# A two-layer outlook-attention kernel on one core: layer 0's fold by SBUF to SBUF transfers instead of shift matmuls, and layer 1's contractions two steps later

## The chip, the cores and the metric

The kernel runs on one core of a Trainium2 chip. The metric is the device time of one execution in microseconds (us). Three runs of the kernel before gave 3605.92, 3610.51 and 3612.76 us; their median, 3610.51 us, is the time before.

## The reference, cut to what matters

Input x is (8, 56, 56, 384) in float32. Two layers follow one another, each with a residual: `x = x + layer(groupnorm(x))`, with 32 groups and statistics per image.

```python
# layer 0: 12 heads of 32, kernel 3x3, attention of 9 outputs over 9 inputs at each pixel
v_unf = patches of v = x @ Wv.T, padded by 1        # (b, n, 9, heads, 32)
a = (x @ Wa.T).reshape(b, n, heads, 9, 9)
attn = softmax(a * 32 ** -0.5)                      # over the 9 inputs q
out = einsum('bnhpq,bnqhd->bnphd', attn, v_unf)
canvas[:, i:i+h, j:j+w] += out[:, :, :, p]          # for the 9 outputs p = (i, j): a fold
return canvas[1:-1, 1:-1] @ Wo.T

# layer 1: 6 heads of 64, one output per pixel, so no fold
a = softmax((x @ W_attn + b_attn).reshape(B, H*W, 6, 9))
y = einsum('bpKhd,bphK->bphd', patches of x @ W_v + b_v, a)
return y @ W_proj + b_proj
```

In layer 0 a pixel's nine outputs land on its 3x3 neighbourhood, and each of them reads a 3x3 neighbourhood: weights of one pixel on another reach over 5x5. The kernel first adds up these weights (over columns, then over rows: "presum" and "fold") and applies them once to v.

## The kernel before, in words

**Layout.** Two images make a pair (`NPAIR` 4); a column of a pair is `R` = 112 rows (2 x 56). Layer 0 walks 4 x 56 = 224 columns, one a step. Eight patches of seven columns (`PX` 7) make an image's width; a patch is contracted when all the columns that reach into it are ready.

**A step of layer 0** (the loop at L677) does this, for different columns:

- `attend(c)`: three projections by `wa_t` into one of three PSUM banks (matmuls of 288 columns), each followed on DVE by a maximum (L486) and a subtraction (L487), with one piece of other work ("between") after each; then the exponential on ACT (L491), a projection by `wv_t` into a bank, its copy `v` on ACT (L498) and `v`'s write to a table in HBM (`vtab`, ACT's DMA queue), the denominator on DVE (L503 to L509) and the multiplication on POOL (L510).
- `presum(c)` for the column two steps back: on POOL, the weights of columns c-1, c and c+1 that land on the same column offset are added into `pre` (5 offsets x 12 heads, for the 9 row pairs pi, qi).
- `fold(c)` for the column three steps back, as the second of the three "between" pieces: the row part. Two matmuls with a 0/1 matrix `shift` move qi = 0 and qi = 2 up and down by one row and add them over pi - qi in PSUM (`pw`, L549); ACT copies the outer two of the five row offsets (L555) and DVE adds qi = 1 to the inner three (L556) into `wt`. `wt` is wider than a patch and zero around the middle, so that a shifted window of it is the row for a patch; L561 writes one such window per patch that the column reaches (336 windows in all) to a table in HBM, `ztab`, as five runs of 336 bytes a row, on ACT's DMA queue.
- `jobs.run`: up to two jobs from a list with due steps.

For each patch `fetch_v` reads the v rows (`vp`, two transfers) and `fetch` the weight rows (`z`, two transfers of 2352 KB, then the residual `xres`), all on SP's DMA queue. `fetch` adds ten jobs, due four steps later: four contractions (96 matmuls `pc` each, with two copies `yT` by ACT) and six output projections (`po`, DVE adds the residual, SP stores to `x1s`). So five steps of seven have two jobs and two have none.

**Layer 1** (the loop at L932) walks 32 groups of seven columns. `attend` projects one tile a step (logits and v, L777) and writes v to a table; at m = 0 `regroup` sends the logits of the group before through HBM; at m = 2 `weigh` makes the softmax (DVE, ACT, at last POOL at L824); at m = 3 `move` shifts by matmuls (`pw`), copies and writes `ztab1`, and `fetch` reads `vp` and `z` and adds the contractions, due four steps later. `load` (L718) brings a group's input at m = 4, `normed` normalises it at m = 6. Inputs `x1t` stay until the group is written out: four buffers, three of `io` and the one that was layer 0's `xres`. The weight tiles `z` are four halves of layer 0's two `z` buffers (`NZ` 4).

**What sets the order.** TensorE's instructions stay in the order of the program (`tc.keep_in_program_order`). Every other instruction is ordered, engine by engine, by a planner that estimates when each can start; DMAs too, on the queue of the engine that issues them (SP or ACT). DMAs take eight completion semaphores in turn, and a DMA waits for the one that had its semaphore before it, so the ninth waits for the first.

Of the kernel before, what the change touches and what calls it, by code (L numbers as in the profile page):

```python
# [15 lines left out]
def two_outlook_layers(  # L16
# [67 lines left out]
    WT = 2 * SX0 - E0  # L84
# [295 lines left out]
    def layer0(late, pools):  # L380
# [6 lines left out]
        stats, st1s, params, xins, attns, pres, xrs, xts = {}, {}, {}, {}, {}, {}, {}, {}  # L387
# [7 lines left out]
        def stats_chunk(pair, blk, i, alone):  # L395
# [16 lines left out]
            if i == NCH - 1:  # L412
                nc.sync.dma_start(
                    xTs[pair][:, :, blk * XB * R : (blk + 1) * XB * R], xt.rearrange("p i m r -> p i (m r)")
                )
                del xrs[pair, blk], xts[pair, blk]
# [13 lines left out]
        wts = [fixed.tile([R, E0, WT, HEADS0], F32, name=f"wt0_{n}") for n in range(NWT)]  # L430
        for wt in wts:
            nc.vector.memset(wt, 0.0)

# [79 lines left out]
        def presum(pair, c):  # L513


            pre = work.tile([R, K2, E0, HEADS0], F32, tag="pre", name=f"pre_{pair}_{c}")

            def of(t, f, n):

                a = attns.get((pair, c + t))  # L520
                if a is None:
                    return None
                a = a.rearrange("r pi (qi qj) (pj h) -> r (pi qi) qj pj h", qj=K, pj=K)
                return a[:, :, 1 - t, f - 1 - t : f - 1 - t + n, :]

            def put(f, n, *terms):
                dst, terms = pre[:, :, f : f + n, :], [t for t in terms if t is not None]
# [9 lines left out]
            put(2, 1, pre[:, :, 2:3, :], of(1, 2, 1)) if c + 1 < W else None  # L537
# [3 lines left out]
            pres[pair, c] = pre  # L541

        def fold(pair, c):


            pre = pres.pop((pair, c)).rearrange("r (pi qi) f h -> r pi qi (f h)", qi=K)
            pw = ps.tile([R, E0, E0 * HEADS0], F32, tag="f", name=f"pw_{pair}_{c}")
            for qi in (0, 2):
                matmul(  # L549
                    pw[:, 2 - qi : 2 - qi + K, :], shift[:, qi, :], pre[:, :, qi, :],  # L550
                    start=(qi == 0), stop=(qi == 2), skip_group_check=True,
                )
            wt = wts[c % NWT]
            mid = wt[:, :, SX0 - E0 : SX0, :].rearrange("r e f h -> r e (f h)")
            nc.scalar.copy(mid[:, 0 : E0 : E0 - 1, :], pw[:, 0 : E0 : E0 - 1, :])  # L555
            nc.vector.tensor_tensor(mid[:, 1 : 1 + K, :], pw[:, 1 : 1 + K, :], pre[:, :, 1, :], ALU.add)  # L556

            for px, sx in patches_of(c, 2):
                lo = SX0 - 1 - sx
                at = sx * SLOT0 + FIRST0 * ROW0  # L560
                nc.scalar.dma_start(  # L561
                    ztab0[(pair * NPX + px) % NTAB][MARGIN : MARGIN + R, at : at + E0 * ROW0].rearrange("r (e w) -> r e w", e=E0),
                    wt[:, :, lo : lo + PX, :].rearrange("r e m h -> r e (m h)"),
# [113 lines left out]
        for step in range(NPAIR * W + LAG):  # L677
# [3 lines left out]
            if step >= LAG:  # L681
                todo.insert(1, lambda: fold(*divmod(step - LAG, W)))
# [4 lines left out]
            while todo:  # L687
                between()

# [21 lines left out]
    def layer1(pools, base, last_of_layer0, late_w):  # L711
# [5 lines left out]

        def load(g):  # L718
            pair, px = divmod(g, NPX)

            if g % 4 == 3:
                t = late_w.tile([P, NCH, T], F32, tag="xres", name=f"x1t_{g}")
            else:
# [4 lines left out]
        def normed(g, m0, m1):  # L728
# [31 lines left out]

        NZ = 4
        half_z = NPY1 * PY1 * ROW1
        zs1 = [
            zs[n // 2].rearrange("p n e -> p (n e)")[: SX1 * SY1, n % 2 * half_z : (n % 2 + 1) * half_z]
            .rearrange("p (n e) -> p n e", n=NPY1)
            for n in range(NZ)
        ]
# [86 lines left out]

        def fetch(g, due):
# [7 lines left out]
            for b in range(IMG):  # L863
                z, vp = zs1[(g * IMG + b) % NZ], vps[b]
                bands(
                    nc.sync, z, ztab1[g % NTAB], LINE1, SLOT1, ROW1, MARGIN - 1, GROUPS1,
                    b, PY1, NPY1,
                )
# [138 lines left out]
```

## Time and profile before

| what | value |
|---|---|
| runs | 3605.92, 3610.51, 3612.76 us (median 3610.51) |
| profiled execution, its own time | 3612.74 us |
| span of its profile | 3610.8 us (1.9 us lie around it) |
| mean granted TensorE clock | 0.978 |
| busy: PE, PEld, DVE, ACT, POOL | 3460.6, 2375.8, 1914.9, 1165.1, 986.4 us |
| layer 0's loop, 100 to 2330 us: PE, DVE, ACT, POOL busy; DMA share | 2218.2, 1526.8, 688.9, 922.4 us; 0.79 |
| layer 1, 2430 to 3540 us: PE, DVE, ACT, POOL busy; DMA share | 1049.8, 306.2, 395.7, 28.4 us; 0.79 |

The profile comes from one execution. "Busy" is the time in which an engine executes; the DMA share is the mean busy share of the core's 16 DMA engines. A group line gives line, engine, operation, out<-in, shape and count, then busy time and the mean of one, then the engine's idle time ahead of these instructions and what ended it. In a timeline each row is a run of like instructions of one engine; a bracket gives the idle time ahead and what ended it. In the stage before 100 us and around 2330 to 2430 us the layers begin and change over.

### The profile page before, as it was taken

To read this page: it belongs to the slowest core of one execution; us is meant where nothing else is said; L and a number is where in the kernel's file an instruction comes from. 1 tells how busy PE (TensorE), PEld (TensorE's weight loads), DVE (VectorE), ACT (ScalarE), POOL (GpSimd) and SP (SyncE) were. 2 spreads that over 40 slices of the span, in tenths; PEclk is the share of its full clock that TensorE was granted. 3 is DMA by queue.
4 is the path that set the end of the run, shared out by engine and by line. 5 is a ranking of instruction groups with operands and counts; after the bars stand their busy time and mean duration, and the time that the engine had idled before them with its cause. 6 is when DMAs were issued, how large, how long until landed. Compare 5 with 4: busy or idle time off the path is not lost.

```text
span 3610.8 us, 72232 instructions
## 1 busy us (share of the span) xinstructions
PE 3460.6 (96%) x29078; PEld 2375.8 (66%) x29078; DVE 1914.9 (53%) x4648; ACT 1165.1 (32%) x2727; POOL 986.4 (27%) x1409
## 2 busy tenths in 40 slices
PE   4999999999999999999999999989999999999998
PEld 4667767777777777777767777655565565556555
DVE  3766666667666676667666666532222222222222
ACT  2333322332333333333222322232333433333332
POOL 2444334434444434443444444410000000000000
PEclk6999999999999999999999999999999999999999
DMA  9799988688886778887667777677778787777876
GB/s 294 202 285 292 267 265 257 226 249 263 267 271 208 263 238 254 261 258 262 204 208 241 218 223 231 222 252 188 207 200 220 206 226 196 199 218 198 219 196 159
DMA packets 692253, 840.73 MB, mean 233 GB/s; under 512 B 302222, under 2 KB 596174, under 8 KB 687822
## 3 DMA queue, kind: packets, MB, share of 16 engines
q1 hardware_dynamic: 329614, 576.00, 51.1%
q10 hardware_dynamic: 362304, 260.11, 27.5%
q8 instruction: 229, 3.75, 0.5%
q14 instruction: 106, 0.87, 0.1%
HBM read 514.32 MB, written 321.66 MB: 232 GB/s over the span
## 4 chain that ended last, share of the span: by engine, by line
PE 78%; DMA 16%; DVE 2%; ACT 1%; issue 1%; POOL 1%; ACTq 0%; SPq 0%; POOLq 0%; DVEq 0%
PE bank L119 44%; PE po L119 15%; PE pc L119 11%; DMA ztab<-wz 5%; PE pw L119 4%; DMA z<-ztab 3%; DMA lgtab<-lgt 2%; PE pt L122 2%; DMA at<-lgtab 1%; DMA xr<-in_x 1%; PE bank L122 1%; DMA vtab<-v 1%; DMA x1t<-x 1%; DMA xT<-xt 1%; DMA vp<-vtab 1%
## 5 line engine op out<-in xcount | busy, mean ns | idle before, releaser
L119 PE MATMUL bank<-wa_t,xn 128*112 128x288 f32 x4032 | 1083.6, 408 | 2.2 <-ACT xn L471 2.2
L119 PEld LDWEIGHTS bank<-wa_t,xn 128*112 128x112 f32 x4032 | 691.9, 177 | 253.1 <-issue 31.9
L510 POOL TENSOR_TENSOR at<-at,den 112x972 f32<-112x972 f32 x224 | 504.9, 2254 | 1226.6 <-DVE den L509 1181.7
L119 PE MATMUL po<-yT,wo_t 128*128 128x448 f32 (+1 forms) x2304 | 823.7, 497 | 5.4 <-DVE x1t L621 4.8
L119 PEld LDWEIGHTS po<-yT,wo_t 128*128 128x128 f32 x2304 | 435.3, 192 | 296.2 <-issue 192.2
L119 PE MATMUL pc<-z,vp 121*32 121x49 f32 (+1 forms) x17664 | 490.0, 255 | 50.6 <-DMA z<-ztab 23.1
L119 PEld LDWEIGHTS pc<-z,vp 121*32 121x32 f32 (+1 forms) x17664 | 444.2, 131 | 127.5 <-issue 91.8
L119 PE MATMUL bank<-wc_t,xn 128*128 128x438 f32 x1176 | 485.7, 549 | 3.8 <-DMA wc_t<-in_wv 2.6
L486 DVE TENSOR_REDUCE mx<-bank 112x36 f32<-112x324 f32 x672 | 327.1, 487 | 299.5 <-PE bank L119 292.9
L119 PE MATMUL bank<-wv_t,xn 128*128 128x384 f32 x1176 | 418.6, 492 | 0.0
L824 POOL TENSOR_TENSOR at<-at,den 112x378 f32<-112x378 f32 x32 | 30.2, 945 | 1142.4 <-DVE den L823 704.8
L487 DVE TENSOR_TENSOR at<-bank,mx 112x324 f32<-112x324 f32 x672 | 328.5, 489 | 21.1 <-DVE mx L486 0.5
L491 ACT ACTIVATE at<-at 112x972 f32<-112x972 f32 x224 | 227.1, 1014 | 331.7 <-DVE at L487 307.9
L119 PEld LDWEIGHTS bank<-wc_t,xn 128*128 128x128 f32 x1176 | 216.3, 193 | 177.9 <-issue 167.2
L740 ACT ACTIVATE xn<-x1t,bias,scale 128x168 f32<-128x168 f32 (+4 forms) x498 | 213.6, 503 | 322.1 <-DMA x1t<-x 227.9
L119 PEld LDWEIGHTS bank<-wv_t,xn 128*128 128x128 f32 x1176 | 219.5, 191 | 139.5 <-issue 18.6
L899 DVE SCALAR_TENSOR_TENSOR x1t<-po,bo_t,x1t 128x448 f32<-128x448 f32 (+1 forms) x192 | 120.1, 626 | 339.6 <-PE po L119 339.6
L555 ACT COPY wt<-pw 112x120 f32<-112x120 f32 x224 | 58.0, 259 | 662.1 <-PE pw L119 577.5
L533 POOL TENSOR_TENSOR pre<-at,at 112x108 f32<-112x108 f32 (+1 forms) x440 | 238.0, 541 | 115.0 <-DVE wt L556 100.6
L779 DVE TENSOR_TENSOR lgt<-bank,ba_t 128x54 f32<-128x54 f32 x196 | 41.1, 210 | 417.2 <-PE bank L119 417.1
L503 DVE TENSOR_TENSOR d<-at 112x432 f32<-112x432 f32 x224 | 141.1, 630 | 196.9 <-ACT at L491 196.9
L600 ACT COPY yT<-pc 128x294 f32<-128x294 f32 x256 | 103.3, 408 | 372.1 <-PE pc L119 318.8
(81 smaller groups left out, 2845.4 us busy)
## 6 DMA issues: line engine op xcount, KB each, us to landing
z<-ztab SPq DMA_DIRECT2D x64, 2352.0 KB
vp<-vtab SPq DMA_DIRECT2D x64, 1536.0 KB
ztab<-wt ACTq DMA_DIRECT2D x336, 183.8 KB
vp<-vtab SPq DMA_DIRECT2D x64, 945.0 KB
xT<-xt SPq DMA_DIRECT2D x56, 672.0 KB
xin<-xT ACTq DMA_DIRECT2D x56, 672.0 KB
xres<-xT SPq DMA_DIRECT2D x32, 1176.0 KB
x1t<-x SPq DMA_DIRECT2D x32, 1176.0 KB
```

The lines of the kernel that those rows point to most:

```text
L119: tc.keep_in_program_order(nc.tensor.matmul(*args, **kwargs))
L122: tc.keep_in_program_order(nc.tensor.transpose(*args, **kwargs))
L486: nc.vector.tensor_reduce(mx[:, pi, :], pl.rearrange("r q a -> r a q"), AX.X, ALU.max)
L487: nc.vector.tensor_tensor(at[:, pi], pl, mx[:, pi, :].unsqueeze(1).to_broadcast([R, K2, PH]), ALU.subtract)
L491: nc.scalar.activation(at, at, AF.Exp, scale=SCALE0)
L503: nc.vector.tensor_add(d4, at[:, :, 0:4], at[:, :, 4:8])
L510: nc.gpsimd.tensor_tensor(at, at, den.unsqueeze(2).to_broadcast([R, K, K2, PH]), ALU.mult)
L533: nc.gpsimd.tensor_tensor(dst, terms[0], terms[1], ALU.add)
L555: nc.scalar.copy(mid[:, 0 : E0 : E0 - 1, :], pw[:, 0 : E0 : E0 - 1, :])
L600: nc.scalar.copy(yT[:, :, :, b, rows_of], pc.rearrange("p i n y m -> p i m (n y)"))
L740: nc.scalar.activation(to[:, i, :, rows], x1ts[g][:, i, lo - first : hi - first, rows], AF.Identity, bias=bias[:, i, b : b + 1], scale=sca ...
L899: nc.vector.scalar_tensor_tensor(res, po[:, :n], bo_t[:, j : j + 1], res, ALU.add, ALU.add)
```

## The change

In layer 0, `fold` has no matmuls. `presum` writes to one of two fixed tiles `pre_t`, laid out with qi outermost, and then issues two SBUF to SBUF transfers on SP's queue, which copy qi = 0 one row up and qi = 2 one row down (720 bytes a row) into `moved_t`. `fold` runs for the same column as before, but at the end of the step; for each patch that the column reaches, ACT writes rows 2 to 4 from the one and rows 0 and 1 from the other (with a factor `keep` that is 0 at the border between the two images), DVE adds row 2 of the other and then the unmoved part, all straight into a tile `wt` of exactly a patch's width (two per patch parity). POOL clears cells of `wt` that the next column leaves unused. The table write is one run of 1680 bytes a row.

In layer 1, `move` and the reads of `z` (now `fetch_bands`) come at m = 4 instead of 3, `fetch` with the contractions at m = 5 (due four steps after that), `load` at m = 2 instead of 4. Inputs have five buffers, the fifth being the last half of the old `z` buffers; `z` has three halves (`NZ` 3). The loop has two more steps at its end. In the first stage the stores of `xT` on SP keep the program's order.

```diff
-    WT = 2 * SX0 - E0
...
-                nc.sync.dma_start(
+                store = nc.sync.dma_start(
                     xTs[pair][:, :, blk * XB * R : (blk + 1) * XB * R], xt.rearrange("p i m r -> p i (m r)")
                 )
+                if alone:
+                    tc.keep_in_program_order(store)
...
-        wts = [fixed.tile([R, E0, WT, HEADS0], F32, name=f"wt0_{n}") for n in range(NWT)]
+        wts = [
+            [fixed.tile([R, E0, PX, HEADS0], F32, name=f"wt0_{k}_{n}") for n in range(NWT)]
+            for k in range(2)
+        ]
+        held = {}
+        pre_t = [fixed.tile([P, K, K, E0, HEADS0], F32, name=f"pre_{n}") for n in range(NWT)]
+        moved_t = [fixed.tile([P, 2, K, E0, HEADS0], F32, name=f"moved_{n}") for n in range(NWT)]
...
         def presum(pair, c):
-            pre = work.tile([R, K2, E0, HEADS0], F32, tag="pre", name=f"pre_{pair}_{c}")
+            whole = pre_t[c % NWT]
+            pre = whole[:R].rearrange("r qi pi f h -> r pi qi f h")
...
-            pres[pair, c] = pre
+            up = moved_t[c % NWT]
+            nc.sync.dma_start(up[:R, 0], whole[1 : 1 + R, 0])
+            nc.sync.dma_start(up[1 : 1 + R, 1], whole[:R, K - 1])
 
         def fold(pair, c):
-            pw = ps.tile([R, E0, E0 * HEADS0], F32, tag="f", name=f"pw_{pair}_{c}")
-            for qi in (0, 2):
-                matmul(
-                    pw[:, 2 - qi : 2 - qi + K, :], shift[:, qi, :], pre[:, :, qi, :],
-                    start=(qi == 0), stop=(qi == 2), skip_group_check=True,
-                )
-            wt = wts[c % NWT]
-            mid = wt[:, :, SX0 - E0 : SX0, :].rearrange("r e f h -> r e (f h)")
-            nc.scalar.copy(mid[:, 0 : E0 : E0 - 1, :], pw[:, 0 : E0 : E0 - 1, :])
-            nc.vector.tensor_tensor(mid[:, 1 : 1 + K, :], pw[:, 1 : 1 + K, :], pre[:, :, 1, :], ALU.add)
+            pre, up = pre_t[c % NWT][:R, 1], moved_t[c % NWT][:R]
             for px, sx in patches_of(c, 2):
-                lo = SX0 - 1 - sx
+                f0, f1 = max(0, E0 - 1 - sx), min(E0, PX + E0 - 1 - sx)
+                m0, m1 = sx - E0 + 1 + f0, sx - E0 + 1 + f1
+                wt = wts[px % 2][sx % NWT]
+                old = held.get((px % 2, sx % NWT), range(0))
+                stale = [m for m in old if not m0 <= m < m1]
+                if stale:
+                    nc.gpsimd.memset(wt[:, :, stale[0] : stale[-1] + 1, :], 0.0)
+                held[px % 2, sx % NWT] = range(m0, m1)
+                to = wt[:, :, m0:m1, :]
+                nc.scalar.activation(to[:, 2:], up[:, 0, :, f0:f1, :], AF.Copy, scale=keep[:, 0:1])
+                nc.scalar.activation(to[:, :2], up[:, 1, :2, f0:f1, :], AF.Copy, scale=keep[:, 1:2])
+                nc.vector.scalar_tensor_tensor(
+                    to[:, 2], up[:, 1, 2, f0:f1, :], keep[:, 1:2], to[:, 2], ALU.mult, ALU.add
+                )
+                nc.vector.tensor_tensor(
+                    to[:, 1 : 1 + K], to[:, 1 : 1 + K], pre[:, :, f0:f1, :], ALU.add
+                )
                 at = sx * SLOT0 + FIRST0 * ROW0
                 nc.scalar.dma_start(
-                    ztab0[...][MARGIN : MARGIN + R, at : at + E0 * ROW0].rearrange("r (e w) -> r e w", e=E0),
-                    wt[:, :, lo : lo + PX, :].rearrange("r e m h -> r e (m h)"),
+                    ztab0[...][MARGIN : MARGIN + R, at : at + E0 * ROW0],
+                    wt.rearrange("r e m h -> r (e m h)"),
                 )
...
             todo = [lambda: jobs.run(step, 1)] * 2
-            if step >= LAG:
-                todo.insert(1, lambda: fold(*divmod(step - LAG, W)))
...
             while todo:
                 between()
+            if step >= LAG:
+                fold(*divmod(step - LAG, W))
...
+        NZ = 3
+        half = NPY0 * PY0 * ROW0 // 2
+        halves = [z.rearrange("p n e -> p (n e)")[:, n * half : (n + 1) * half] for z in zs for n in range(2)]
         def load(g):
-            if g % 4 == 3:
+            if g % 5 == 3:
                 t = late_w.tile([P, NCH, T], F32, tag="xres", name=f"x1t_{g}")
+            elif g % 5 == 4:
+                t = halves[3][:, : NCH * T].rearrange("p (i t) -> p i t", i=NCH)
...
+        def fetch_bands(g):
+            for b in range(IMG):
+                bands(
+                    nc.sync, zs1[(g * IMG + b) % NZ], ztab1[g % NTAB], LINE1, SLOT1, ROW1, MARGIN - 1,
+                    GROUPS1, b, PY1, NPY1,
+                )
...
-        for step in range(NG * PX + 4):
+        for step in range(NG * PX + 6):
...
-            if m == 4 and g + 1 < NG:
+            if m == 2 and g + 1 < NG:
                 load(g + 1)
...
-            if g and m == 3:
+            if g and m == 4:
                 move(g - 1)
                 while not clear_bands.done:
                     jobs.run(None, 1)
+                fetch_bands(g - 1)
+            if g and m == 5:
                 fetch(g - 1, base + step + 4)
```

## The prediction, made before the changed kernel ran

> **What bounds the kernel now.** I read the page's busy line first, then the sums by stage, then TensorE's timeline within a step, then the waits.
>
> ```profile
> PE 3460.6 (96%) x29078; PEld 2375.8 (66%) x29078; DVE 1914.9 (53%) x4648; ACT 1165.1 (32%) x2727; POOL 986.4 (27%) x1409
> PEclk6999999999999999999999999999999999999999
> ```
>
> TensorE (PE) is busy nearly all the time. The view by stages says where it is not (columns: length, then busy us of PE, weight loads, DVE, ACT, POOL, the granted clock, DMA share, GB/s):
>
> ```profile
> 100.00:2330.00 2230.00, 2218.24 (x19456) 1587.88 (x19458) 1526.81 (x3774) 688.91 (x1351) 922.42 (x1331) 1.00 0.79 245
> 2430.00:3540.00 1110.00, 1049.82 (x7925) 654.35 (x7925) 306.15 (x659) 395.68 (x1188) 28.36 (x30) 0.98 0.79 205
> ```
>
> In layer 0 PE is idle 12 us of 2230: what PE has to do sets that stage, and a matmul taken away there shortens it. In layer 1 it is idle 60 us of 1110, at a clock of 0.98. What one fold takes of PE is seen from start to start in its timeline:
>
> ```profile
> 1003.38 1.71 PE L119 MATMUL bank<-wa_t,xn 128*112 128x288 f32 x6
> 1004.93 0.78 PE L119 MATMUL pw<-pre,shift 112*112 112x180 f32 x4
> 1005.54 1.62 PE L119 MATMUL bank<-wa_t,xn 128*112 128x288 f32 x6
> 1007.09 2.33 PE L119 MATMUL pc<-z,vp 121*32 121x49 f32 x96
> ...
> 1017.13 0.78 PE L119 MATMUL pw<-pre,shift 112*112 112x180 f32 x4
> 1017.74 1.62 PE L119 MATMUL bank<-wa_t,xn 128*112 128x288 f32 x6
> ```
>
> 1004.93 to 1005.54 is 0.61 us, and a step with jobs takes 1017.13 - 1004.93 = 12.2 us. Before the first contraction, without jobs, the folds start 7.3 us apart (118.70, 126.09, 133.39). Last, PE's own waits, and in layer 1 what they end on:
>
> ```profile
> PE pw L119 <- POOL at L824: 27.4, 16, 3.7
> PE pc L119 <- DMA z<-ztab: 23.1, 12, 4.5
> ```
>
> Both are layer 1's: the softmax not ready for `move`, the weights not there for the contraction. Going through layer 1's PE gaps one by one gives 24.9 + 26.7 = 51.6 of its 60 idle us to these two.
>
> **What the Trainium skill says.** "DMA: Bandwidth & Descriptors", section "Queues, rings and completion order": SP and ACT each own one row of rings, and each DMA engine consumes a ring's descriptors in order. The trace agrees. At 1049.07 SP issues two `z` reads; their packets run from 1050.1 to 1066.4, those of `xres` (issued 1056.2) from 1065.5 to 1069.9 and of the next store (1060.0) from 1068.8 to 1073.9. Same page, "Anatomy of one DMA": a wait for a semaphore is made by the issuing sequencer, so a waiting DMA holds up what its engine has behind it; SP's queue waits 683.9 us in all on `vtab<-v` ahead of `vp`. Same page, "Specifications": below 512 bytes a transfer loses rate; here a 336-byte packet took 25 ns and a 1344-byte one 62 ns, so four times the bytes took 2.5 times as long. "TensorE: Matmul & The Clock Gate", Part 1: about 3.4 us of idleness halves the clock. Agrees: after a 4.5 us wait at 2427, 48 `pc` take 2.30 us instead of 1.61 and the next `bank` group 3.37 instead of 2.47.
>
> **The change part by part.**
>
> *Matmuls removed.* 224 folds x 0.61 us = 137 us of PE's queue, none of it hidden, as PE is the bound. The short waits of `pw` for `pre` (3.0 + 3.9 us, single gaps of layer 0) go too: -7. Sum -144.
>
> *ACT and DVE.* The copy (L555, 259 ns) and the addition (L556, 341 ns) go. Per column come 1.5 patches, each with two ACT and two DVE operations. ACT: rows of 294, 384 and 448 elements take 408, 472 and 533 ns, so about 0.16 us + 0.8 ns an element; 3 operations with 300 elements make 0.48 + 0.25 = 0.73, +0.47 us a column. DVE: 108 and 432 elements take 0.26 and 0.63 us, so about 0.13 us + 1.15 ns; 3 operations with 240 elements make 0.67, +0.33 us a column. By column DVE then has 1527/224 + 0.33 = 7.1 us and ACT 3.1 + 0.5 = 3.6 of a mean step of 9.3 us (2230/224 - 0.61). Both stay below PE: nothing on the path, from work alone. If the cover went, DVE's part is 75 us. POOL's clearing (at most one 120-element piece a patch, some 0.2 us by the 108-element `MEMSET` of 188 ns) stays under 4.1 + 0.4 us a column.
>
> *DMA.* Table writes: 187,600 packets x 25 ns / 16 engines = 297 us fall away; 37,600 x about 80 ns (1792 bytes took 85) / 16 = 188 us come. The new transfers: 50,176 packets of 720 bytes, between the 31 ns of a 504-byte write and the 68 of an 840-byte read, 97 to 213 us; I take 130. Together +20 of 16 engines' time: nothing.
>
> *The new wait*, the part no row of before shows. `fold` on ACT now waits for `moved`. Behind it in ACT's queue are the exponential, the copy of `v` (frees a bank) and the copies `yT` (free `pc`); behind DVE's part are the maxima that free banks. PE waits for these. Time to the data: from the end of column c+1's exponential (999.6) through the denominator and POOL's product (to 1005.99) to the last piece of `pre` (1007.06) is 7.5 us; on an idle SP queue I add 3.5 us (the small `at<-lgtab` read ended 2.1 us after its issue, plus issue and waits). So 11 us after exponential c+1. The planner's new order places ACT's part of `fold` after exponential c+2 in 115 columns, after c+3 in 44, already after c+1 in 63. With steps of 6.7 (no jobs) and 11.6 us, the first two have slack; the third makes the exponential 2 to 4 us late. PE has three banks, and DVE needs that exponential only after it has freed the next column's first bank: some 5 us of cover, so nothing, if such columns don't pile up.
>
> Behind the `z` pair it is longer. The planner has put the next `moved` after `z`, `z`, `xres`: it lands 22 us after `z` is issued (17 + 4 + 1). I place `z` about 1 us after exponential c+1 (c the first column behind it), since the table write of column c-2 must land first. Its fold stands after exponential c+3, about 11.4 + 9 us after exponential c+1, and before the next, 6.8 us on: 23 against 26. It fits, by 3 us; DVE's part sits about 1 us tighter. So the bounds are 0 and, if a few us are missing in each of the 32 patches, 4 x 32 = 128 us. There is no gain in it. I take 40 us (1.25 us a patch), since transfers of SP and ACT also wait on each other over eight semaphores: some 7 DMAs a step instead of 5 (448 more over 224 steps) make one turn of them last 10 us instead of 15, less than a `z` or `xres` takes.
>
> *Layer 1 later.* `move` gets one step more (5.4 us) behind `weigh`; the waits for POOL were at most 3.7 us: gone. `z` keeps its distance to `move`, but contractions come five steps after it instead of four; waits were at most 4.5 us: gone, unless `z`'s third half isn't free. That needs the former group's first two contractions, which end in the step before: free. The two steps earlier for `load` only take waits off ACT (`xn` on `x1t`, 227.9 us, no PE time seen). Of 51.6 us I take 45. The clock lost 2% of 1110 = 22 us to restarts after these waits; I take 8, between 0 and 22. SP's order has the same transfers, `z` before or after `vp` alike. The two extra steps at the end only shift work that PE has anyway: 0, at most 5.
>
> *Sum.* -144 + 40 - 45 - 8 = -157 on the profiled execution's 3612.7 (span 3610.8 and 1.9 around it): 3455.7; that execution lay 2.2 us above the median: **3454 us**.
>
> **The rivals.**
>
> *A, the forecast:* PE keeps the lead, 3410 (no new wait) to 3510. For it: 96% and the planner's spacing behind `z`.
>
> *B, the new waits eat most of it.* 4 us a patch instead of 1.25: 3454 - 40 + 128 = 3542; 3510 to 3600. For it: SP's queue holds packets half the time (q1 51.1% of the engines), `vp` too stands between two `moved`. Against: PE's three banks.
>
> *C, slower: behind `z` and `xres` `moved` comes late in every patch,* ACT and DVE stand, PE follows. The gain is 3611 - 3414 = 197 us without new waits, so it decides from 197/32 = 6.2 us a patch that PE stands. If each late `moved` delays two columns by 4 us, 8 x 32 = 256: 3670. For it: my margin is 3 us, `z` pairs took 15 to 26 us. Against: steps behind `z` have no contractions, so little is queued for ACT.
>
> *D, layer 1's waits stay* (the table write `ztab<-wz`, 10 to 15 us in the chain, grows with the delay): 3454 + 53 = 3507.
>
> That the change doesn't do what it says is excluded by the new order: PE has 448 matmuls fewer and `pw` stands a step later.
>
> **How the numbers follow.** A 0.58, B 0.16, C 0.17, D 0.09. Likeliest 3454, A's own range 3410 to 3510. The range for 8 in 10 runs from 3412 to B's 3575: C and the last of B lie above. Faster by over 0.2% (7 us, about what a measurement of this kernel can tell from no change): A, B nearly whole and D, 0.81; within 0.2% the edge of B, 0.03; slower 0.16.
>
> **What would show it.** Right: layer 0's loop 95 to 145 us shorter at PE over 97% busy, no `pw` there; layer 1 with PE idle under 20 us. Wrong: PE waits for ACT `yT` or `v` or DVE `at` in clusters some 20 us after each `z` issue, with ACT waiting for DMA `moved<-pre` (B, C); `pc` waiting for `z` in layer 1 (D).

## The result, and the profile after

The changed kernel takes 3801.09 us (median of 4 runs, 3779.02 to 3806.46) against 3610.59 us for the kernel before on the same chip: a ratio of 1.0518, 95% interval 1.0474 to 1.0562. The forecast was 3454 us, a gain of 157; the changed kernel is slower than the kernel before, by 190 us. The profiled execution took 3797.61 us with a span of 3795.9.

From the page of the changed kernel, the busy line and the clock that TensorE was granted:

```profile
PE 3431.1 (90%) x28182; PEld 2278.5 (60%) x28182; DVE 2114.3 (56%) x5102; ACT 1298.1 (34%) x3175; POOL 1041.5 (27%) x1656
PEclk5999999999999999999999999989999999999999
```

The matmuls are gone (28,182 for 29,078), and PE is busy 29.5 us less, where 137 us were taken from it: the matmuls that are left took some 107 us longer. Most of that, some 90 us, fits the clock: 0.952 over the span where it was 0.978, and 2.6% of 3460 us are 90. It is lower in both layers, as the view below shows; why was not tested by itself. PE's idle time, span minus busy, went from 150.2 to 364.8 us. So -137 for matmuls, +107 for slower ones and +215 of idle time make the +185 us between the two spans.

The view by stages, with layer 1's window moved along (columns as in the prediction):

```profile
100.00:2330.00 2230.00, 2041.62 (x17562) 1392.18 (x17564) 1637.39 (x3993) 778.63 (x1707) 920.16 (x1483) 0.97 0.75 248
2630.00:3740.00 1110.00, 1028.78 (x7553) 641.27 (x7552) 290.49 (x633) 378.59 (x1129) 26.42 (x28) 0.96 0.77 199
```

In layer 0, where PE was idle 12 us of 2230, it now is idle 188, and in the same stretch it gets through 17,562 matmuls for 19,456, of which 888 were the fold's. In layer 1 it is idle 81 us for 60. The waits of the whole run say on what (us in total, times, longest):

```profile
ACT wt L582 <- DMA moved<-pre: 528.4, 139, 10.2
DVE mx L848 <- DMA at<-lgtab: 200.2, 32, 9.0
PE po L118 <- DVE x1t L651: 131.7, 57, 5.7
DVE wt L584 <- DMA moved<-pre: 101.8, 44, 5.8
PE pc L118 <- ACT yT L916: 81.3, 41, 5.2
PE pc L118 <- ACT yT L630: 37.0, 28, 6.3
PE bank L118 <- DVE at L506: 34.9, 31, 3.3
```

Layer 1's old waits, `pw` for POOL and `z` for the table, are indeed gone; `pc` for the copy `yT` (L916) has come instead. In layer 0 PE waits for DVE's residual addition `x1t`, for DVE's subtractions and for ACT's `yT`. ACT and DVE stand for `moved`: the instruction at the head of their queue waits for the transferred rows, and all behind it waits too. How one becomes the other is seen in the timeline of the changed kernel's layer 0 (start, length, engine, line; in brackets the wait before):

```profile
1011.94 0.35 ACT L582 ACTIVATE wt<-moved,keep 112x72 f32<-112x72 f32 x1 [7.00 <-DMA moved<-pre]
...
1012.57 0.24 DVE L584 SCALAR_TENSOR_TENSOR wt<-moved,keep,wt 112x24 f32<-112x24 f32 x1 [3.86 <-DMA moved<-pre]
...
1013.33 0.48 DVE L505 TENSOR_REDUCE mx<-bank 112x36 f32<-112x324 f32 x1
...
1016.60 0.50 DVE L506 TENSOR_TENSOR at<-bank,mx 112x324 f32<-112x324 f32 x1
...
1017.13 1.01 ACT L510 ACTIVATE at<-at 112x972 f32<-112x972 f32 x1 [0.79 <-DVE at L506]
...
1018.18 0.61 DVE L522 TENSOR_TENSOR d<-at 112x432 f32<-112x432 f32 x1 [1.08 <-ACT at L510]
...
1021.73 0.61 DVE L651 TENSOR_TENSOR x1t<-po,xres 128x448 f32<-128x448 f32 x1
1021.96 2.24 POOL L529 TENSOR_TENSOR at<-at,den 112x972 f32<-112x972 f32 x1 [1.79 <-DVE den L528]
1022.27 1.96 DVE L584 SCALAR_TENSOR_TENSOR wt<-moved,keep,wt 112x12 f32<-112x12 f32 x1
...
1022.40 1.96 PE L118 MATMUL po<-yT,wo_t 128*128 128x336 f32 x6 [1.71 <-DVE x1t L651]
```

DVE stands 3.86 us for the moved rows; its maxima, then ACT's exponential, then the sums of the denominator follow late one behind the other; `x1t`, which frees the only `po` buffer, is behind all of them, and PE waits 1.71 us. The line at 1022.27 shows a second thing: an addition of 12 elements that takes 1.96 us, as long as POOL's multiplication runs beside it.

### The profile page after: what moved, and what is told of

The parts are those of the page before. It is cut to its first block, busy times and chain, and to the rows that moved or that the text cites. A ratio compares the mean times of both kernels' runs of the same rounds, so it can differ in the third digit from the quotient of the medians.

```text
span 3795.9 us, 72859 instructions
## 1 busy us (share of the span) xinstructions
PE 3431.1 (90%) x28182; PEld 2278.5 (60%) x28182; DVE 2114.3 (56%) x5102; ACT 1298.1 (34%) x3175; POOL 1041.5 (27%) x1656
## 5 line engine op out<-in xcount | busy, mean ns | idle before, releaser
L118 PE MATMUL bank<-wa_t,xn 128*112 128x288 f32 x4032 | 1097.3, 415 | 18.1 <-DVE at L506 16.0
L118 PE MATMUL po<-yT,wo_t 128*128 128x448 f32 (+1 forms) x2304 | 858.8, 514 | 137.1 <-DVE x1t L651 131.7
L118 PEld LDWEIGHTS bank<-wa_t,xn 128*112 128x112 f32 x4032 | 705.3, 180 | 327.6 <-issue 64.8
L529 POOL TENSOR_TENSOR at<-at,den 112x972 f32<-112x972 f32 x224 | 504.9, 2254 | 626.7 <-DVE den L528 514.2
L118 PE MATMUL pc<-z,vp 121*32 121x49 f32 (+1 forms) x17664 | 501.6, 257 | 129.4 <-ACT yT L916 81.3
L118 PEld LDWEIGHTS pc<-z,vp 121*32 121x32 f32 (+1 forms) x17664 | 454.1, 134 | 209.2 <-ACT yT L916 92.4
L118 PE MATMUL bank<-wc_t,xn 128*128 128x438 f32 x1176 | 509.0, 571 | 7.4 <-DMA wc_t<-in_wv 7.4
L582 ACT ACTIVATE wt<-moved,keep 112x108 f32<-112x108 f32 (+4 forms) x336 | 128.5, 389 | 597.1 <-DMA moved<-pre 528.4
L584 DVE SCALAR_TENSOR_TENSOR wt<-moved,keep,wt 112x36 f32<-112x36 f32 (+4 forms) x336 | 168.4, 506 | 246.7 <-ACT wt L582 141.8
L777 ACT ACTIVATE xn<-x1t,bias,scale 128x168 f32<-128x168 f32 (+4 forms) x402 | 169.3, 502 | 208.0 <-DMA x1t<-x 188.1
L490 ACT ACTIVATE xn<-xin,bias,scale 128x224 f32<-128x224 f32 x336 | 172.4, 564 | 189.5 <-PE bank L118 136.4
```

Source lines behind the costliest of these rows:

```text
L118: tc.keep_in_program_order(nc.tensor.matmul(*args, **kwargs))
L490: nc.scalar.activation(to[:, i, :, rows], xin[:, i, :, rows], AF.Identity, bias=bias[:, i, b : b + 1], scale=scale[:, i, b : b + 1],)
L529: nc.gpsimd.tensor_tensor(at, at, den.unsqueeze(2).to_broadcast([R, K, K2, PH]), ALU.mult)
L582: nc.scalar.activation(to[:, 2:], up[:, 0, :, f0:f1, :], AF.Copy, scale=keep[:, 0:1])
L584: nc.vector.scalar_tensor_tensor(to[:, 2], up[:, 1, 2, f0:f1, :], keep[:, 1:2], to[:, 2], ALU.mult, ALU.add)
L777: nc.scalar.activation(to[:, i, :, rows], x1ts[g][:, i, lo - first : hi - first, rows], AF.Identity, bias=bias[:, i, b : b + 1], scale=sca ...
```

## The experiments

The expectations number their theories. For layer 0: 1, the two jobs of a step now stand close together; 2, ACT and DVE stand for the transfers (2a: because the planner puts the fold too early in their queues); 3, DVE's additional operations, held up by POOL's, are too much for it; 5, the loop of DVE, ACT and POOL lies just behind PE in any case. For layer 1: 4, the contractions meet the softmax. Ratios are to the kernel before on the same chip, with their 95% interval. PE's idle time in layer 0, where no stretch is given, is counted from 100 us to layer 1's first projection: 20 us in the kernel before, 211 in the changed one.

### Which layer

e1 is the changed layer 0 with the old layer 1, e2 the reverse; no line is altered.

> The changed layer 0 with layer 1 as it was. The two profiles, cut where the layers meet, put about 120 us of the 190 us loss into layer 0 and about 65 into layer 1. Theory (both layers lose, each by its own mechanism): 3611 + 120 = about 3735, between 3715 and 3760. Rival, the prediction's own step on layer 1 (its part is a gain of some 53 us, and all the loss and more is layer 0's): 3801 + 53 = about 3855.

Measured: 3707.37 us, 1.0319 (1.0279 to 1.036).

> Layer 0 as it was with the changed layer 1. Theory (the contractions now share their step with the softmax's wait on ACT, so pc waits for the copy yT): 3611 + 65 = about 3675, with some 75 us of pc waits for yT in layer 1 and hardly any for pw and z. Rival, the prediction's step: 3611 - 53 = 3558, with PE idle under 20 us in layer 1. A third: layer 1's loss comes only from what layer 0 leaves behind in queues and clock; then it stays within 15 us of 3611.

Measured: 3637.90 us, 1.0125 (1.0097 to 1.0154). Both layers lose. The two ratios add up to 1.044; the 0.7% missing to 1.0518 isn't accounted for.

### Layer 1: contractions one step sooner

```diff
-                fetch(g - 1, base + step + 4)
+                fetch(g - 1, base + step + 3)
```

> Layer 0 as it was with the changed layer 1 (that pair took 1.0125 of the kernel before), contractions due one step sooner, so that they begin in step 1 of a patch and not in step 2, where the softmax stands. Theory 4 (contractions meet the softmax's wait on ACT): pc's waits for the copy yT fall from 66 us to under 25 and the ratio to 1.00 or below. Rival (they meet whatever ACT does in any step, since ACT stands behind the load of x1t and the logits): they stay over 45 us, ratio 1.008 to 1.015. A third, that z then comes late: pc waits for z over 20 us.

Measured, on the old layer 0: 3536.55 us, 0.9836 (0.981 to 0.9861). The waits of e2:

```profile
DVE mx L818 <- DMA at<-lgtab: 180.4, 31, 8.9
ACT ot L915 <- DVE at L819: 93.8, 13, 9.0
PE pc L119 <- ACT yT L886: 67.6, 45, 4.4
```

and of e8:

```profile
DVE mx L818 <- DMA at<-lgtab: 50.3, 25, 10.5
PE pc L119 <- ACT yT L886: 3.2, 5, 1.3
```

One number, 4 to 3, turns +45 us into -59. After 2450 us PE is idle 7 us with it and 73 without. In e2 the softmax's maximum (`mx`) stands for the read of the logits from HBM (`lgtab`), ACT's copy of an output (`ot`) stands for DVE, and `yT` is queued behind it. In the changed kernel one sees it at a glance:

```profile
2923.07 0.83 DVE L848 TENSOR_REDUCE mx<-at 112x42 f32<-112x378 f32 x1 [9.03 <-DMA at<-lgtab]
...
2925.35 0.48 ACT L945 COPY ot<-pt 112x384 f32<-112x384 f32 x1 [8.54 <-DVE at L849]
2925.72 0.44 ACT L916 COPY yT<-pc 128x336 f32<-128x336 f32 x1
...
2926.22 2.17 PE L118 MATMUL pc<-z,vp 90*64 90x56 f32 x36 [3.95 <-ACT yT L916]
```

Theory 4 holds in its result, not in its words. Going through e8's contractions by their distance from the maximum, they still run beside the softmax, from 6 us ahead of it to 10 behind; what is gone is the maximum's stand (5.6 us before each in e2, 1.6 in e8). Why the logits come earlier against DVE's queue there was not isolated.

> The whole changed kernel with layer 1's contractions due one step sooner. Theory 4: layer 1's part then is worth what it was worth on the old layer 0 (1.0125 to 0.9836), so 1.052 falls to about 1.023 (1.015 to 1.030), with pc waits for yT in layer 1 under 15 us. Rival (with the changed layer 0 ahead of it ACT and the queues are in another state): a gain under 0.015.

Measured, with the same line in the whole changed kernel: 3669.55 us, 1.0224 (1.0189 to 1.0259), as theory 4 had it.

### Layer 0: spacing, transfers, work

```diff
-            todo = [lambda: jobs.run(step, 1)] * 2
+            todo = [lambda: jobs.run(step, 1), lambda: None, lambda: jobs.run(step, 1)]
```

> The changed kernel with the second job of a step put back behind the third projection, as it was when the fold stood between the two. Theory 1 (two output projections now follow each other with only one projection between them, and the single po buffer isn't free): po's waits for DVE x1t fall from 126 us to under 30, and the time from 3801 by 100 to 160 us, clock included: 3640 to 3700. Theory 2 (ACT and DVE stand waiting for the transfers, and x1t is late for that): within 40 us of 3801, with the waits only moved to other places. Theory 3 (DVE's additions are held up while POOL's multiplication of the probabilities runs): likewise most of the waits stay, since the collision has nothing to do with the place of the job; 3740 to 3801.

Measured: 3746.24 us, 1.0414 (1.0387 to 1.0441). `po`'s waits fell from 132 to 92 us, those of the banks rose from 35 to about 68: in part moved, not gone. The gain is 1.0%, and PE is still idle 192 us in layer 0.

```diff
-                todo.insert(1, lambda: fold(*divmod(step - LAG, W)))
+                todo.insert(2, lambda: fold(*divmod(step - LAG, W)))
```

> The kernel before with its fold's matmuls put behind the third projection, so that the step's two jobs have one projection between them as in the changed kernel, and nothing else. Theory 1 (two output projections so close find the single po buffer taken): po waits for DVE x1t rise from 5 to over 40 us and the ratio is 1.008 or more. Rival (close jobs only hurt where DVE is late for other reasons): po waits under 20 us, ratio within 0.996 to 1.004.

Measured, on the kernel before: 3602.42 us, 1.0034 (1.0019 to 1.0049), `po` waiting about 6 us. Theory 1 falls as the cause by itself: close jobs cost little where DVE is on time.

```diff
-            pre, up = pre_t[c % NWT][:R, 1], moved_t[c % NWT][:R]
+            pre, up = pre_t[c % NWT][:R, 1], pre_t[c % NWT][:R, 0::2]
```

> The changed kernel with the fold's ACT and DVE operations reading the unshifted sums instead of the transferred ones, so that they wait for POOL alone; the transfers are still issued, but nothing waits for them. This leaves out the shift by one row of two of the three row terms. Theory 2 (standing for the transfers is the loss in layer 0): ACT's waits for the transfers, 528 us, go, PE's 212 idle us of layer 0 fall under 70, and the time comes to 3610 to 3670. Theory 1 (job spacing): the 126 us of po waits stay over 100, the yT waits (37 us) go; 3745 to 3801. Theory 3 (DVE against POOL): the po waits stay over 60, 3700 to 3780.

Measured: 3746.15 us, 1.0421 (1.0398 to 1.0444), with PE idle 192 us in layer 0. ACT now stands 713 us for POOL's sums instead of 528 for their transfer. The gain is some 0.010, so the stand wasn't for the transfer alone. But the run doesn't price the transfer cleanly: POOL still has to wait until a transfer has read its sums before it overwrites them, 315 us here for 48 in the changed kernel, and so makes its sums later.

```diff
+            one = inside[:, 1, 0:1]
+            for px, sx in patches_of(c, 2):
...
+                nc.scalar.activation(to[:, 2:], of(0), AF.Copy, scale=one)
+                nc.scalar.activation(to[:, :2], of(2, slice(0, 2)), AF.Copy, scale=one)
+                nc.vector.scalar_tensor_tensor(to[:, 2], of(2)[:, 2], one, to[:, 2], ALU.mult, ALU.add)
+                nc.vector.tensor_tensor(to[:, 1 : 1 + K], to[:, 1 : 1 + K], of(1), ALU.add)
```

> The kernel before, with the changed fold's two ACT and two DVE operations per patch added on spare tiles, of the same shapes and from sums that are ready: their work without their wait for a transfer, and with the matmuls kept. The prediction's step (nothing on the path from work alone): within 10 us of the kernel before. Theory 3 (DVE is too full, its two-input operations stand while POOL multiplies): DVE busy up by 150 to 200 us, PE idle time in layer 0 up by 60 to 150 us, ratio 1.015 to 1.04. Theory 2a: at most 1.006.

Measured: 3656.07 us, 1.017 (1.0149 to 1.0192), DVE 223 us busier, PE idle 58 us in layer 0 for 20. It doesn't decide: the planner put the added operations ahead of their sums too (ACT stood 586 us for POOL in them), so it isn't work alone.

```diff
-                nc.vector.scalar_tensor_tensor(
-                    to[:, 2], up[:, 1, 2, f0:f1, :], keep[:, 1:2], to[:, 2], ALU.mult, ALU.add
-                )
-                nc.vector.tensor_tensor(
+                nc.scalar.activation(up[:, 1, 2, f0:f1, :], up[:, 1, 2, f0:f1, :], AF.Copy, scale=keep[:, 1:2])
+                nc.gpsimd.tensor_tensor(to[:, 2], to[:, 2], up[:, 1, 2, f0:f1, :], ALU.add)
+                nc.gpsimd.tensor_tensor(
                     to[:, 1 : 1 + K], to[:, 1 : 1 + K], pre[:, :, f0:f1, :], ALU.add
                 )
```

> The changed layer 0 with layer 1 as it was (1.032 of the kernel before), and the fold's two additions per patch moved from DVE to POOL, with one more short ACT operation that masks the third row. Theory 3 (DVE's added and slowed operations are the price): DVE's busy time falls by some 300 us, PE's idle time in layer 0 from 195 to under 110 us, ratio 1.005 or less. Theory 2 (whoever folds stands for the transfers): POOL now stands for them as well, the sums come later, idle time stays over 170 and the ratio at 1.03 or above.

Measured: 3749.03 us, 1.0452 (1.0415 to 1.0488): slower than e1, though DVE is busy 1850 us instead of 2121. Theory 3 as the whole cause falls: with that work off DVE, PE still waits 122 us for `x1t`. POOL, which does the additions now, stands 308 us for ACT's part of the fold, as theory 2 had it.

### Layer 0: the matmuls taken away, and nothing put in

```diff
-            pw = ps.tile([R, E0, E0 * HEADS0], F32, tag="f", name=f"pw_{pair}_{c}")
-            for qi in (0, 2):
-                matmul(
...
-            nc.scalar.copy(mid[:, 0 : E0 : E0 - 1, :], pw[:, 0 : E0 : E0 - 1, :])
-            nc.vector.tensor_tensor(mid[:, 1 : 1 + K, :], pw[:, 1 : 1 + K, :], pre[:, :, 1, :], ALU.add)
+            nc.scalar.copy(mid[:, 0 : E0 : E0 - 1, :], pre[:, 0:2, 0, :])
+            nc.vector.tensor_tensor(mid[:, 1 : 1 + K, :], pre[:, :, 2, :], pre[:, :, 1, :], ALU.add)
```

> The kernel before without the fold's four matmuls and nothing put in their place: ACT copies and DVE adds straight from the unshifted sums, where they stood (this leaves out the shift by one row, and of the two outer rows one term). The prediction's first step (-144 us, since PE sets layer 0): 0.960 of the kernel before, PE idle in layer 0 still under 30 us. Theory 5 (the loop of DVE, ACT and POOL through a step lies only a little behind PE; once PE's step is 0.6 us shorter it sets the pace): a gain of at most 80 us, ratio 0.978 or more, with PE waiting over 50 us in layer 0 for DVE and ACT.

Measured: 3658.45 us, 1.0193 (1.0158 to 1.0228). There is less for the bounding engine to do and no new operation on any other, and it is slower. e9's waits:

```profile
DVE wt L550 <- POOL pre L531: 468.4, 203, 3.6
PE po L119 <- DVE x1t L615: 92.1, 73, 3.3
PE bank L119 <- DVE at L487: 65.2, 55, 3.0
```

DVE stands 2.3 us in nearly every column (203 of 224) for POOL's sums. A column of e9:

```profile
1011.26 0.25 DVE L509 TENSOR_TENSOR den<-den,inside 112x108 f32<-112x108 f32 x1
...
1012.24 0.50 DVE L487 TENSOR_TENSOR at<-bank,mx 112x324 f32<-112x324 f32 x1
1012.79 0.62 PEld L119 LDWEIGHTS bank<-wv_t,xn 128*128 128x128 f32 x3 [2.34 <-DVE at L487]
...
1014.70 0.27 POOL L531 COPY pre<-at 112x108 f32<-112x108 f32 x1
...
1015.00 0.77 DVE L550 TENSOR_TENSOR wt<-pre 112x180 f32<-112x180 f32 x1 [2.27 <-POOL pre L531]
...
1015.70 0.48 DVE L486 TENSOR_REDUCE mx<-bank 112x36 f32<-112x324 f32 x1
```

The fold's addition stands one maximum behind the denominator, with which POOL only begins; from there to the end of the sums it is 3.5 us (1011.51 to 1014.97). Counting the maxima in DVE's order between the denominator of column c+1 and the fold of c: one in 168 of 223 columns in e9, four or five in 179 in the kernel before, where the addition also needs `pw`, and `pw`'s place is fixed by PE's program order. So the matmul looks like the fold's anchor, which e13 puts to the test. (The addition also takes longer, 761 ns on average for 341, now that both its operands lie in SBUF.) From here on, cause (a) is the fold's place in the queues, cause (b) that the other engines have no room for a shorter step wherever it stands. e13 restores that place without the matmul; exponential, copy `v` and the fold's own copy and addition are wrapped in the same way:

```diff
-                nc.vector.tensor_tensor(
-                    at[:, pi], pl, mx[:, pi, :].unsqueeze(1).to_broadcast([R, K2, PH]), ALU.subtract
-                )
+                tc.keep_in_program_order(nc.vector.tensor_tensor(
+                    at[:, pi], pl, mx[:, pi, :].unsqueeze(1).to_broadcast([R, K2, PH]), ALU.subtract
+                ))
```

> The kernel before without the fold's matmuls (1.019 of the kernel before when nothing held the fold's place; it leaves out the shift by one row and one outer row term), with ACT's copy kept behind the copy v of its step and DVE's addition kept behind the second subtraction of column c+3, where the matmul had held them. Cause (a), the place: PE's idle time in layer 0 falls from 165 to under 60 us and the ratio to between 0.955 and 0.975, as the prediction had it for the matmuls alone. Cause (b), no room on the other engines: idle stays over 110 us, ratio 0.99 or more.

Measured: 3460.26 us, 0.9634 (0.9612 to 0.9655), PE idle 32 us in layer 0 for 173 in e9. Four or five maxima stand ahead of the addition again (164 columns). In e13 `x1t` waits for PE again (27 us in e9), and of its fold only ACT's part still waits for POOL, no longer DVE's (1 us):

```profile
DVE x1t L615 <- PE po L119: 105.8, 125, 13.2
ACT wt L549 <- POOL pre L531: 134.8, 37, 8.6
```

This settles (a) against (b) in the plain case: order alone is worth 5.6%, and the matmuls are worth 131 us (3.66% of 3593), once the order is kept. Nor was it the longer addition, which takes 960 ns in e13. The same places with the matmuls kept were not run; with PE idle 20 us in layer 0 of the kernel before, they could add little there.

### The changed layer 0, with a place

e5 keeps the fold behind the exponential and denominator of column c+3 (the six operations wrapped as above). e6 does so one column later with three buffers.

> The changed layer 0 with layer 1 as it was (that pair took 1.032 of the kernel before), and the fold's two ACT and two DVE operations held in program order behind the exponential and the denominator of column c+3. Theory 2a (the planner places the fold so early that ACT, and DVE behind it, stand for sums which POOL has not made yet, and through ACT's exponential this loop of DVE, POOL and transfer sets the pace): ACT's waits for the transfers fall from some 500 us to under 200, PE's idle time in layer 0 from 212 to under 120 us, and the ratio to 1.00 or below. Theory 3 (DVE's additional operations, slowed by POOL's, are too much for DVE wherever they stand): idle time stays over 170 us and the ratio between 1.02 and 1.04. If POOL, which now has to wait longer for its two buffers, becomes the wait: POOL waits for DVE wt over 500 us and the ratio stays too.

Measured: 3694.91 us, 1.0282 (1.0257 to 1.0307). ACT's waits for `moved` fell to 171 us as theory 2a had it, but the ratio didn't follow: POOL now waits 574 us in all for DVE's part of the fold (368 in e1), as the last alternative had it.

```diff
-        LAG = 3
+        LAG = 4
...
-            whole = pre_t[c % NWT]
+            whole = pre_t[c % 3]
```

> As the run before it, with the fold one column later (behind column c+4) and three buffers each for the sums and the transferred rows, so that POOL is not held up by the later fold; some constants of layer 1 are made at its start to make room. Theory 2a: hardly any standing of ACT and DVE is left, PE's idle time in layer 0 under 80 us, and with 137 us of matmuls gone the ratio is 0.97 to 0.99. Theory 3: idle time stays over 150 us, ratio 1.015 to 1.035.

Measured: 3671.20 us, 1.0214 (1.0186 to 1.0242). At each change of pair this version overwrites the last two columns' sums before they are folded, which alters values there but not the operations. The stands for `moved` are nearly gone in e6 (ACT's 520 us in e1 are 54; it stands 122 us for POOL's sums), PE's idle time in layer 0 isn't (184 us for 209 in e1). Behind the denominator the additions fall into POOL's multiplication. The group of the addition in e6, and then in e14 (described next), where it stands ahead of the denominator's sums (busy us, mean ns):

```profile
L575 DVE TENSOR_TENSOR wt<-wt,pre 112x108 f32<-112x108 f32 (+4 forms) x336 | 278.1, 828 | 9.8 <-ACT wt L571 1.0 <-DVE wt L572 0.5 <-ACT xn L478 0.5
```

```profile
L601 DVE TENSOR_TENSOR wt<-wt,pre 112x108 f32<-112x108 f32 (+4 forms) x336 | 123.6, 368 | 41.7 <-ACT wt L586 2.0 <-DVE wt L596 1.4 <-POOL pre L553 0.5
```

e14 cuts the fold in two, `fold_rows` and `fold_add`, with its operations wrapped as above: ACT's part after the exponential and `v` of column c+2, DVE's between the last subtraction and the first sum of c+3. e15 is e14 with the changed layer 1 and its `step + 3`, e16 also has the old spacing.

```diff
+            job = lambda: jobs.run(step, 1)
+            rows = lambda: fold_rows(*divmod(step - LAG, W)) if step >= LAG else None
+            todo = [job, lambda: [rows(), job()]]
...
                 between()
+            fold_add()
             nc.scalar.activation(at, at, AF.Exp, scale=SCALE0)
```

> The changed layer 0 with layer 1 as it was (1.032 of the kernel before), and the fold cut in two with a fixed place for each: ACT's part behind the exponential of column c+2, DVE's part between the last subtraction and the first sum of column c+3, where POOL is through with its multiplication. Cause (a): PE's idle time in layer 0 falls from 195 to under 90 us and the ratio to 0.995 or less. Cause (b), with DVE's additional and slowed operations: idle time stays over 140 us and the ratio over 1.015.

> As the run before it, with the changed layer 1 and its contractions one step sooner, which was worth 0.016 on the old layer 0. So 0.016 below the run before it: under 0.98 by cause (a), over 1.00 by cause (b).

> As the run before it, with the step's second job behind the third projection. Moving the jobs together cost 0.003 on the kernel before (1.0034) and moving them apart gained 0.010 on the changed one (1.0518 to 1.0414). If the spacing costs by itself: 0.003 to 0.010 below the run before it, po waits for x1t halved. If it only cost where DVE was late: within 0.003 of it.

Measured: e14 3809.91 us, 1.06 (1.0565 to 1.0635); e15 3756.71 us, 1.0468 (1.044 to 1.0497); e16 3749.01 us, 1.0444 (1.0419 to 1.047). Given a place, the changed layer 0 is slower than without (e14 against e1's 1.0319), with PE idle 298 us in e14: the ratios are those of cause (b). Yet PE hardly waits for DVE any more. The waits for `x1t` went, as cause (a) would have it (130 us in e1, 12 in e16), and another came. From e16:

```profile
PE bank L118 <- ACT v L518: 267.2, 43, 14.6
PE po L118 <- DVE x1t L666: 11.8, 10, 3.3
```

Of the waits for `v`, 217 us end between 20 and 30 us after the issue of a `z` pair, in 23 of the 32 patches. The last two runs follow them: e17 lets POOL issue the transfers, e18 also has ACT clear the stale cells.

```diff
-            nc.sync.dma_start(up[:R, 0], whole[1 : 1 + R, 0])
-            nc.sync.dma_start(up[1 : 1 + R, 1], whole[:R, K - 1])
+            nc.gpsimd.dma_start(up[:R, 0], whole[1 : 1 + R, 0])
+            nc.gpsimd.dma_start(up[1 : 1 + R, 1], whole[:R, K - 1])
```

> As e16 (1.044), with the two transfers of the moved rows issued by POOL itself, behind its last sum, and not by SP behind z, xres and vp. If SP's order is what is left (the prediction's rival C, some 8 us in each patch): waits for ACT v fall from 263 to under 60 us, PE's idle time in layer 0 from 271 to under 90, and the ratio to 0.96 to 0.99. If the transfers are late in any queue, since the z packets fill the DMA engines: v waits stay over 150 us and the ratio over 1.01.

Measured: 3623.22 us, 1.0108 (1.0087 to 1.0129), with 99.5 us of waits for `v`, of which 16 us still lie 20 to 30 us after a `z` pair. Issuing the transfers from POOL's queue instead of SP's, behind `z`, is worth 3.4% here, and isn't all: PE is idle 175 us in layer 0.

```diff
-                    nc.gpsimd.memset(wt[:, :, stale[0] : stale[-1] + 1, :], 0.0)
+                    old = wt[:, :, stale[0] : stale[-1] + 1, :]
+                    tc.keep_in_program_order(nc.scalar.activation(old, old, AF.Copy, scale=0.0))
```

> As e17 (1.0108), with the stale columns cleared by ACT (a copy times zero, ahead of its two parts of the fold) and not by POOL. If POOL's stand for the table write is the rest: POOL's waits for it (397 us) are gone, ACT's for the moved rows (639 us) fall by half or more, PE's idle time in layer 0 from 161 to under 80 us, ratio 0.96 to 0.985. If the transfers' own latency is the rest: v waits stay over 80 us, ratio over 1.00.

Measured: 3620.31 us, 1.0086 (1.0055 to 1.0118); the interval overlaps e17's. POOL's 405 us of standing in the clearing are gone and next to nothing is won, so hardly anybody waited for them. Still, in e18:

```profile
ACT wt L584 <- DMA moved<-pre: 634.1, 156, 11.1
PE bank L118 <- ACT v L518: 91.0, 53, 6.2
```

From the end of exponential c+1 until both transfers of `moved` for column c are issued it is 9.0 us in e18 (median), against a median step of 9.6 us: ACT's part, one exponential later, is still too early once the transfer's own time is added.

## Why the prediction was wrong, point by point

**Matmuls, -144.** Right in size: 131 us in e13. Wrong in "none of it hidden, as PE is the bound": taken away alone they cost 1.9% (e9), since they also held the fold's place in the queues of ACT and DVE.

**ACT and DVE, "nothing on the path, from work alone".** It compared means (7.1 of 9.3 us a column). The changed kernel's DVE is 199 us busier, not 75. The price had no term for additions that start while POOL multiplies; by the figures in the last section they are held up for some 165 us. e10 took that work off DVE and won nothing, e7 couldn't part it from its place; what the work alone costs stays open.

**DMA, nothing.** Right: the table writes went from 298 to 191 us of the 16 engines' time, the transfers took 121.

**The new wait, 40 us of 0 to 128.** This is the step that failed in layer 0. e1 loses 115 us where 131 were to be had, so waits and slower matmuls cost 246 us. "The first two have slack" was read from ACT's order alone, with the 11 us to the data about right (both transfers are issued 9.3 us after exponential c+1, median in the changed kernel). But in the 115 columns where ACT's part follows exponential c+2, only 1.3 us (median) pass from the first issue to the end of that exponential, and ACT stood 139 times. DVE's order was read only as far as the maxima that free the banks, and the five us of cover of the three banks say nothing on `x1t`, which sits in the same queue with a single buffer behind it.

**Behind `z`.** The changed kernel's own waits are not gathered there (of PE's 211 idle us in layer 0, 29 lie 20 to 30 us after a `z` pair's issue); rival C, as priced, wasn't the cause. It shows once the fold has a fixed place: 217 us in e16, of which 16 are left when POOL issues the transfers (e17).

**POOL's clearing, nothing.** Right, as far as e18 against e17 shows, where ACT clears instead.

**Layer 1, -45 and -8.** The waits named did go, and layer 1 alone still lost 1.25%. The step that failed is "contractions come five steps after it instead of four" as a pure gain: it asked whether `z` is there, not what ACT and DVE stand for in the steps into which the copies `yT` move. With contractions four steps after `move`, as in the kernel before, the sum of -53 is met by -59 (e8). That is in part luck: the price put 26.7 us of waits for `z` down to the fifth step, and in e8 they are gone without it, but for one at the layer's start (12 waits before). Why `z` comes in time there was not isolated.

**What stays open.** Each single repair of layer 0 took away 0.4 to 1.1% (e3 to e6), and the versions with the fold cut in two (e14 to e18) still lose; with layer 1's 0.9836 divided out, e18's layer 0 is at 1.025. e6 has few stands (ACT's and DVE's parts of the fold wait 197 us for sums and moved rows, 635 in e1) but more collisions with POOL's multiplication (170 of the 672 operations on DVE start beside it, 116 in e1); e14 to e18 have fewer collisions (53 to 86) and most of the stands (522 to 769 us). That the two together are the rest is argued, not shown: a version with three buffers and DVE's part ahead of the denominator was not run. Of all versions that do the whole fold, e8 is the fastest, 1.6% ahead of the kernel before: layer 0 as it was, the changed layer 1, contractions due three steps after `fetch`.

## What to carry to other kernels

An instruction on an engine with a fixed order also fixes when its consumers may start on the engines that a planner orders. Before it is taken away, look in each consumer's queue at what it will be put in front of, and when its data are made; here that decided whether the same matmuls, taken away, won 3.7% or lost 1.9%. When a stage is moved by a step, look at what the engines that evacuate it stand for in the step it moves to.

## What the runs showed of the hardware

DVE operations with two operands in SBUF wait out POOL's multiplication, which itself has two and takes 2254 ns. In the changed kernel 117 of the fold's 672 operations on DVE start while it runs: the 67 multiply-adds then take 1423 ns on average instead of 278, the 50 plain additions 2060 instead of 298, and the multiply-adds over 700 ns all end within 100 ns of its end. The kernel before adds `pw` from PSUM to `pre`; 84 of its 224 additions start beside the same multiplication and take 339 ns, 341 being the mean of all. The Trainium skill, "SBUF — State Buffer", section "SBUF: two separate sides", has the rule: DVE and GpSimd share a pair of ports under an exclusive lock, a DVE operation with two SBUF inputs takes part in it against a GpSimd operation that reads SBUF, whoever starts first has it for the whole instruction, and "the other fully blocks". The times agree with it for DVE; that POOL waits for DVE is not shown here. It need not cost anything: in e13 114 of 224 additions start beside the multiplication, at 1478 ns instead of 422, and the gain of 131 us is there.
